# Where the low halves of three weight tensors are subtracted on GpSimd in a two-layer transformer kernel

## The chip, the cores and the metric

The kernel runs on one core of a Trainium2 chip. The metric is the device time of one execution in microseconds, the median of three. A core has the matrix engine TensorE (PE in the profile, its weight loads PEld), the vector engine VectorE (DVE), the activation engine ScalarE (ACT), GpSimd (POOL), and SyncE (SP), which here issues DMAs. Each engine works through its own list of instructions in order, and semaphores join the lists.

## The reference

Input `x` is 8 batches of 512 rows of 256 values, float32. Two pre-norm layers follow each other, each an attention and a gated feed-forward (FFN):

- layer 0 attention: `x += softmax(causal(q k^T / 4)) v`, 16 heads of width 16, with `q, k, v = layernorm(layernorm(x)) * gamma + beta` times `w_qkv`
- layer 0 FFN: `x += fp4(h) wd^T`, with `h = silu(fp4(y) wg^T) * (fp4(y) wu^T)`, `y = layernorm(x)`; width 704. `fp4` rounds each block of 16 values to a grid of 8 magnitudes times a scale taken from the block's maximum. The weights are rounded in the same way
- layer 1 attention: banded (each row sees 64 rows), with biases and an output projection
- layer 1 FFN: gated, width 768, weights integers times 1/127

## The kernel before

**Halves.** [...] a tensor is split: ACT casts it to `high`, POOL subtracts `low = full - high`, and TensorE forms three products (`PAIRS`: high·high, high·low, low·high). Four sets of such low halves matter here: those of layer 0's gate, up and first input (L969, made in attention), of layer 0's down weights `wd_low` (L1209), of the FFN's inputs `fyT` for batches 1 to 7 (`split`, L289 to L295), and of layer 1's q, k and v weights (`late_weights`, L1177; the trace calls these tiles `qkv_wg` and `qkv_wu`, after the slots they use).

**Attention 0** (about 0 to 501.9 us of the trace) runs over 8 batches × 2 halves × 2 groups = 32 "quads" of four heads. In step `i` of the loop in `body`, quad `i` takes its exponentials and its weighted sums while quad `i + 2` forms scores and row maxima (L506, L517). One step has six parts `p`. `side[p]` holds what else belongs to a part: projections, transposes, finishing the quad before. The exponentials go from PE (L609) through ACT (L620) to POOL, which zeroes the masked triangle (`only`, L128), and back to PE (L674). `fill` is a generator that feeds layer 0's weight rounding into these steps. The layer 1 call of the same function has a second generator, `last_weights`, stepped in the last quads.

**FFN 0** (501.9 to about 800 us) runs over 32 tiles of 128 rows, `n` in the code, four to a batch. Step `n` turns the rows of tile `n-3` (PE L1246, ACT L1250, DVE L1251), forms gate and up for tile `n` (24 matmuls at L1227, ACT silu L1233, DVE product L1234), starts rounding tile `n` (`quantize`: DVE L221, L227, L228, then POOL L229), multiplies tile `n-3` by the down weights (L1260), and ends the rounding of tile `n-1` (ACT L277, DVE L279 and L281, POOL L282). `prepare(b)`, advanced twice a step, normalizes, rounds, transposes and splits the inputs of the next batch, `fy` and then `fyT`. `late_weights` is advanced once a step from `n = 6` on. Its first three steps make the halves of layer 1's q, k and v weights; then it loads `wd2_i`.

**What sets the order.** The framework's scheduler orders each engine's list by its own estimate of when things are ready and how urgent they are; it may move an instruction far from where the program has it. `keep_in_program_order` (called `pin` too) puts an edge from the instruction traced last on the same engine to this one, so that it can't be issued before that. It adds no wait on a result. A tile pool's buffers are known by tags; a new tile with the tag of an old one waits until that is no longer used. The pool `fp` of the FFN takes the memory of attention's pool `ap`, and its first tiles wait for attention's end. `wp` lives through both.

Before the change `wd_high` lies in `wp` under the tag `raw`, in the place of `qkv_raw`, which attention's last projection reads at 440.2 us. `wd_low` lies in `fp`.

Of the kernel before, what the change touches and what calls it, by code (L numbers as in the profile page):

```python
# [10 lines left out]
F32 = mybir.dt.float32  # L11
BF16 = mybir.dt.bfloat16
F32R = mybir.dt.float32r
# [3 lines left out]
ALU = mybir.AluOpType  # L17
AX = mybir.AxisListType

P = 128  # L20
B, S, D = 8, 512, 256
# [25 lines left out]
def tile_two_layers(  # L47
# [22 lines left out]
    nc = tc.nc  # L70
# [4 lines left out]
    wp = tc.alloc_tile_pool(name="weights0", bufs=1, side="right")  # L75
# [23 lines left out]
    qkv_raw = wp.tile([P, NE, 3 * D], F32, tag="raw", name="qkv_raw")  # L99
# [73 lines left out]
    def pin(ins):  # L173

        tc.keep_in_program_order(ins)
# [113 lines left out]
    def split(pool, hi, lo, src, name):  # L289

        n = src.free_size()
        full = pool.tile([P, 512], F32, tag="full", name=f"full_{name}", bufs=1)[:, :n]
        nc.scalar.copy(hi, src)
        nc.scalar.copy(full, src)
        nc.gpsimd.tensor_tensor(lo, full, hi.bitcast(F32), ALU.subtract)  # L295

    def project(dst, lhs, rhs):

# [58 lines left out]

    QK = [units_tiles(qk, n, "both") for n in range(2)]

    def attention(home, banded, stats, norm, spin, wq_s, wk_s, wv_s, qcol, kcol, bv_bc, post, filler):  # L360

# [91 lines left out]
        def load_q(u):  # L455
            HALF[u, 0] = pieces(*u, wq_s, qcol, "q")
# [287 lines left out]
        def body():  # L744

            q, k = units_tiles(home[0], 2, int(banded))
            QQ.append(q)
            KK.append(k)
            padded_values(home[0], 1, nc.gpsimd)
            if banded:  # L750
                for n in range(2):
                    v = home[0].tile([P, NT, H, HP], F32, tag=f"vq{n}", name=f"vq{n}", bufs=1)
                    nc.gpsimd.memset(v[WIN:, 0], 0.0)
                    VQ.append(v)
                shifted(0)
                fine = fine_halves(home[0])
                next(fine)
            norm(1)
            for i in range(1 if banded else 0, 2):
                for s in scores(i):  # L760
                    s()
                maxima(i)
            max_rows(0)
            for c in range(NE):
                turned(1, c)
            load_q(units[2])
            stores(units[2], 0)
            load_k(units[2])
            stores(units[2], 1)
            land(units[2])  # L770


            last = trail = None
            ending = filler(home[0]) if banded else None
            for i in range(len(quads) + (2 if banded else 1)):
                ts, ss, cur = [], [], None
                if i < len(quads):
                    cur = Outputs(i)
                    ts = cur.tiles()
                    if i + 2 < len(quads):  # L780
                        ss = scores(i + 2)
                c, r = i // 4, i % 4
                nT = 2 if banded else 6
                side = {p: [] for p in range(nT)}

                def at(p, fn):
                    side[p].append(fn)

                p1, p2, p3 = (1, 0, 0) if banded else (1, 2, 3)
                f1, f2, f3 = (0, 1, 1) if banded else (0, nT - 2, nT - 1)  # L790
                if banded and i + 1 < len(quads):
                    at(p3, lambda: max_rows(i + 1))

                if last is not None:
                    at(p1, lambda: last.banded_sums() if banded else last.sums((2, 3)))
                    at(p1, lambda: last.copy())
                done = trail if banded else last
                if done is not None and not banded:
                    at(p2, lambda: done.finish())

                if r == 0 and c + 1 < B:
                    at(f2 if banded else f1, lambda: values(c + 1, 0))
                if r == (2 if banded else 0) and c + 1 < B:
                    at(f1 if banded else f2, lambda: values(c + 1, 2))
                if r == 2 and c + 2 < B:
                    at(f3 if banded else f1, lambda: turned(c + 2, 0))
                    at(f3, lambda: turned(c + 2, 1))
                if r == 0 and c + 2 < B:
                    at(f3, lambda: stats(c + 2))
                if r == 1 and c + 2 < B and not banded:  # L810
                    for t in range(NT):
                        at(t, lambda t=t: norm(c + 2, [t]))
                if banded and r == 3 and c + 1 < B:
                    at(f1, lambda: shifted(c + 1))
                if r % 2 and i // 2 + 3 < len(units):
                    at(f1, lambda: load_q(units[i // 2 + 3]))
                    at(f2, lambda: load_k(units[i // 2 + 3]))
                    at(f3, lambda: stores(units[i // 2 + 3], 0))
                for p, fn in tail.pop(i, ()) if banded else ():
                    at(p, fn)  # L820
                if done is not None and banded:
                    at(p2, lambda: done.finish())
                if i + 1 < len(quads) and not banded:
                    at(p3, lambda: max_rows(i + 1))
                if cur and not banded:
                    at(f3, lambda: cur.sums((0, 1)))
                if r == 1 and c + 2 < B and banded:
                    for t in range(NT):
                        at(t // 2, lambda t=t: norm(c + 2, [t]))
                if r % 2 == 0 and i and i // 2 + 2 < len(units):  # L830
                    at(f1 if banded else p1, lambda: stores(units[i // 2 + 2], 1))
                    at(f1 if banded else f2, lambda: land(units[i // 2 + 2]))
                for p in range(max(len(ts), nT if last or done else 0)):
                    if p < len(ss):
                        ss[p]()
                        step()
                    if p < len(ts):
                        ts[p]()
                        step()
                    for fn in side[p]:  # L840
                        fn()
                    if banded and p:
                        next(fine, None)
                    if banded and i > 4 * B - 6:
                        next(ending, None)
                if ss:
                    maxima(i + 2)
                last, trail = cur, last
            for _ in ending or ():
                pass  # L850
            for n in sorted(tail) if banded else ():
                for p, fn in tail.pop(n):
                    fn()
# [6 lines left out]
    NH = (F1 + P - 1) // P  # L860
    wd1 = wp.tile([P, NH, D], F32, tag="wd1", name="wd1")
# [111 lines left out]
    HALVES = {}  # L973
    wqp = tc.alloc_tile_pool(name="wquant", bufs=1, side="right")
    with tc.tile_pool(name="attn0", bufs=2) as ap:
# [6 lines left out]
        fill = before_ffn(wqp)  # L982
# [15 lines left out]
        def spin0(b, c, dst):  # L998
            transposed(dst, Y[b], f"a{b}", [c], (gcol, bcol), True)

        def post0(b, c, o, rz):
            tmp = ap.tile([P, NT, 4, HD], F32, tag="on", name=f"on_{b}_{c}")
            nc.vector.tensor_tensor(tmp, o, rz, ALU.mult)
            xs = X[b][:, :, c * 64 : (c + 1) * 64]
            nc.gpsimd.tensor_tensor(xs, xs, tmp.rearrange("p t j d -> p t (j d)"), ALU.add)

        opening0, body0 = attention(
            (ap, 1, 2, None), False, stats0, norm0, spin0, qkv_raw[:, :, 0:D], qkv_raw[:, :, D : 2 * D],
            qkv_raw[:, :, 2 * D : 3 * D], None, None, None, post0, fill,
        )  # L1010
        for _ in opening0():
            pass
# [9 lines left out]
    bv_bc = const.tile([P, D], F32, tag="bvb", name="bv_bc")  # L1022
# [104 lines left out]
    def last_weights(pool):  # L1127
# [24 lines left out]

    opening1, body1 = attention(
        home1, True, stats1, norm1, spin1, raw1[:, 0], raw1[:, 1], raw1[:, 2], qcol1, kcol1, bv_bc,
        post1, last_weights,
    )
    with tc.tile_pool(name="ffn0", bufs=2) as fp:
        both = []
# [10 lines left out]
        def late_weights():  # L1169
# [4 lines left out]
            ]  # L1174
            for i in range(3):
                nc.scalar.copy(halves[0][:, i], raw1[:, i])
                nc.gpsimd.tensor_tensor(  # L1177
                    halves[1][:, i], raw1[:, i], halves[0][:, i].bitcast(F32), ALU.subtract
                )
                yield  # L1180
            flat = wp.tile([P, 6 * D], I32, tag="wd1", name="wd2_i")
            nc.sync.dma_start(
# [12 lines left out]
        def prepare(b):  # L1195
# [6 lines left out]


        wd_halves = [
            wp.tile([P, NH, D], F32R, tag="raw", name="wd_high"),
            fp.tile([P, NH, D], F32R, tag="wdl", name="wd_low", bufs=1),
        ]
        nc.scalar.copy(wd_halves[0], wd1)
        nc.gpsimd.tensor_tensor(  # L1209
            wd_halves[1], wd1, wd_halves[0].bitcast(F32), ALU.subtract  # L1210
        )


        rows = [fp.tile([P, NH * P], F32, tag=f"h{i}", name=f"h{i}", bufs=1) for i in range(4)]
# [177 lines left out]
    with tc.If(nc.values_load(beyond, min_val=0, max_val=P) != 0):  # L1392
        with tc.tile_pool(name="over", bufs=1) as op:
# [10 lines left out]
            for b in range(B):  # L1404
                y = op.tile([P, NT, D], F32, tag="y", name=f"oy_{b}")
# [63 lines left out]
```

## Time and profile before

| | us |
|---|---|
| three timed runs, median | 1280.49 (1279.89 to 1282.59) |
| the profiled execution's own time | 1288.33 |
| its span in the trace | 1286.5 |
| PE busy | 1100.3 |
| DVE busy | 943.5 |
| POOL busy | 698.8 |
| ACT busy | 659.7 |

A line of the timeline reads: start in us, duration in us, engine, line of the kernel, operation, output `<-` inputs with sizes, how many (`x3`), and in brackets how long the engine had been idle and whose result ended that. When several of one kind follow each other they are merged, and the duration runs from the first start to the last end. A line of the waits reads: who waited, for whom, total in us, times, longest. A line of the windows reads: stretch, its length, busy us and count of PE, PEld, DVE, ACT and POOL, TensorE's granted clock as a share of full speed, and the DMAs' share and rate.

### The profile page before, as it was taken

To read this page: it belongs to the slowest core of one execution; us is meant where nothing else is said; L and a number is where in the kernel's file an instruction comes from. 1 tells how busy PE (TensorE), PEld (TensorE's weight loads), DVE (VectorE), ACT (ScalarE), POOL (GpSimd) and SP (SyncE) were. 2 spreads that over 40 slices of the span, in tenths; PEclk is the share of its full clock that TensorE was granted. 3 is DMA by queue.
4 is the path that set the end of the run, shared out by engine and by line. 5 is a ranking of instruction groups with operands and counts; after the bars stand their busy time and mean duration, and the time that the engine had idled before them with its cause. 6 is when DMAs were issued, how large, how long until landed. Compare 5 with 4: busy or idle time off the path is not lost. (4 is left out here: it accounts for less than half of the span.)

```text
span 1286.5 us, 27214 instructions
## 1 busy us (share of the span) xinstructions
PE 1100.3 (86%) x10910; PEld 819.8 (64%) x10910; DVE 943.5 (73%) x1603; ACT 659.7 (51%) x1008; POOL 698.8 (54%) x821
## 2 busy tenths in 40 slices
PE   4778989788998888788888887788998898889998
PEld 2444444444554445787888777567777776668887
DVE  4699896698788885789799857677776686545553
ACT  3255656465674676444444333455555554455553
POOL 5165564465445566655555533576766675534443
PEclk9899999898998999899999988899999998999999
DMA  8644334443453311000000025476675676000001
GB/s 229 140 96 87 86 74 86 79 94 67 91 116 74 81 18 50 1 1 1 1 1 1 1 72 105 100 165 155 144 149 125 141 164 163 2 1 33 33 26 43
DMA packets 51634, 99.53 MB, mean 77 GB/s; under 512 B 6702, under 2 KB 43568, under 8 KB 44848
## 3 DMA queue, kind: packets, MB, share of 16 engines
q1 hardware_dynamic: 50624, 96.96, 33.9%
q8 instruction: 88, 1.44, 0.5%
q10 hardware_dynamic: 816, 0.79, 0.2%
q14 instruction: 42, 0.34, 0.1%
q0 software_dynamic: 64, 0.00, 0.0%
HBM read 61.02 MB, written 29.36 MB: 70 GB/s over the span
## 5 line engine op out<-in xcount | busy, mean ns | idle before, releaser
L128 POOL TENSOR_SCALAR_AFFINE_SELECT ex<-ex 64x512 f32<-64x512 f32 (+2 forms) x448 | 268.9, 603 | 226.1 <-ACT ex L620 131.3
L620 ACT ACTIVATE ex<-t 128x1024 f32<-128x1024 f32 (+1 forms) x192 | 167.9, 882 | 125.3 <-PE t L609 114.1
L517 DVE TENSOR_REDUCE mx<-s 128x2 f32<-128x1024 f32 (+2 forms) x192 | 196.7, 1036 | 41.1 <-PE s L506 40.3
L1319 POOL TENSOR_TENSOR hT<-gh,hT 128x512 fp32r<-128x512 f32 x48 | 61.6, 1290 | 89.6 <-ACT hT L1318 66.1
L655 ACT ACTIVATE ex<-t 128x1024 f32<-128x1024 f32 x64 | 65.5, 1023 | 86.6 <-PE t L647 81.9
L501 PE MATMUL s<-kk_both,qq_both 96*128 96x512 bf16 (+3 forms) x352 | 84.6, 323 | 20.8 <-DVE mx L517 10.9
L506 PE MATMUL s<-cmask,minus_b 128*128 128x128 bf16 (+2 forms) x352 | 90.4, 257 | 0.0
L540 DVE TENSOR_REDUCE mx<-s 128x8 f32<-128x1024 f32 x64 | 77.6, 1215 | 15.3 <-PE s L535 15.2
L282 POOL TENSOR_TENSOR h<-h,sc_h 128x704 f32<-128x704 f32 x32 | 45.1, 1410 | 79.4 <-DVE h L281 73.6
L674 PE MATMUL po<-ex,vp 128*32 128x512 f32 (+3 forms) x1024 | 83.4, 442 | 1.3 <-DVE kr L418 1.3
L609 PE MATMUL t<-qq_both,kk_both 108*128 108x512 bf16 (+3 forms) x352 | 70.9, 306 | 9.1 <-ACT ex L620 4.7
L1386 DVE SCALAR_TENSOR_TENSOR gh<-ggu,gsl 128x512 f32<-128x512 f32 x48 | 33.2, 691 | 57.1 <-ACT gsl L1384 56.6
L1260 PE MATMUL pd<-wd_high,hT 128*128 128x256 f32 x384 | 61.7, 299 | 11.6 <-DVE hT L1251 7.0
L277 ACT ACTIVATE mg_h<-h 128x704 bf16<-128x704 f32 x32 | 25.2, 788 | 82.7 <-POOL h L229 82.7
L1227 PE MATMUL gu<-wg_wgh,fyT 128*128 128x352 f32 x224 | 65.3, 333 | 2.4 <-DVE h L1234 2.4
L501 PEld LDWEIGHTS <-qq_both 96*128 96x128 bf16 x352 | 33.0, 103 | 51.6 <-issue 38.0
L229 POOL TENSOR_TENSOR h<-h,rc_h 128x704 f32<-128x704 f32 x32 | 46.4, 1449 | 34.1 <-DVE rc_h L228 18.8
L1260 PEld LDWEIGHTS pd<-wd_high,hT 128*128 128x128 f32 x384 | 53.7, 200 | 16.4 <-DVE hT L1251 10.7
L1227 PE MATMUL gu<-wu_wuh,fyT 128*128 128x352 f32 x224 | 62.7, 322 | 0.0
L1375 PE MATMUL ggu<-yT,wg_r 128*128 128x512 f32 x192 | 57.6, 412 | 2.1 <-DVE yT L1319 1.1
L279 DVE SCALAR_TENSOR_TENSOR h<-mg_h,h 128x704 f32<-128x704 bf16 x32 | 40.6, 1269 | 22.4 <-ACT mg_h L277 22.4
L674 PEld LDWEIGHTS po<-ex,vp 128*32 128x32 f32 x1024 | 27.1, 109 | 43.9 <-issue 29.8
(335 smaller groups left out, 3167.9 us busy)
## 6 DMA issues: line engine op xcount, KB each, us to landing
q_hbm<-qp SPq DMA_DIRECT2D x90, 128.0 KB
k_hbm<-kp SPq DMA_DIRECT2D x90, 128.0 KB
qq_both<-q_hbm SPq DMA_DIRECT2D x44, 256.0 KB
kk_both<-k_hbm SPq DMA_DIRECT2D x22, 384.0 KB
qq_both<-q_hbm SPq DMA_DIRECT2D x44, 128.0 KB
kk_both<-k_hbm SPq DMA_DIRECT2D x22, 256.0 KB
qq<-q_hbm SPq DMA_DIRECT2D x20, 256.0 KB
vq<-vp SPq DMA_DIRECT2D x8, 512.0 KB
```

The source lines that it names most:

```text
L128: nc.gpsimd.affine_select(out=t, in_=t, compare_op=ALU.is_ge, fill=0.0, base=base, pattern=[[0, n] for n in shape[1:-1]] + [[sign, shape[- ...
L501: pin(nc.tensor.matmul(bank[:, a * w : (a + 1) * w], lhsT=q[:KF, hs[j], t * P : w], rhs=k[:KF, hs[j], :w], start=(a == 0), stop=False, ski ...
L506: pin(nc.tensor.matmul(bank.rearrange("p (i k) -> p i k", k=w)[:, :, t * P :], lhsT=minus_b, rhs=cmask[:, : len(part), :], start=False, st ...
L517: nc.vector.tensor_reduce(dst, src, AX.X, ALU.max)
L540: nc.vector.tensor_reduce(mx[:, t2 : t2 + 2, :], sc.rearrange("p t (j k) -> p t j k", k=P), AX.X, ALU.max)
L609: pin(nc.tensor.matmul(bank[:, a * w : (a + 1) * w], lhsT=k[: KF + 12, self.hs[j], t * P : (t + 1) * P], rhs=q[: KF + 12, self.hs[j], t * ...
L620: nc.scalar.activation(ex[:, :banks, :used], sc[:, :banks, :used], AF.Exp, scale=QSCALE)
L655: nc.scalar.activation(ex, sc, AF.Exp, scale=QSCALE)
L674: pin(nc.tensor.matmul(self.o[HP * j : HP * (j + 1), t * P :], lhsT=vp[:, t, 4 * c + j, :], rhs=self.ex[t, j], start=(t == 0), stop=(t == ...
L1227: nc.tensor.matmul(gu[:, i, :352], lhsT=YT[b][l][:, e, t * P : (t + 1) * P], rhs=w[r][:, e, f], start=(n == 0), stop=(n == 3 * NE - 1),)
L1260: nc.tensor.matmul(pd[:, :D], lhsT=hT[l][:, k, :], rhs=wd_halves[r][:, k, :], start=(l == r == k == 0), stop=(l == 1 and k == NH - 1),)
L1319: engine.tensor_tensor(lo, src, hi.bitcast(F32), ALU.subtract)
```

## The change

`attention` gets one more argument, a generator stepped in its last quads; layer 0 is given the new `down_low`, layer 1 its `last_weights` as before. `down_low` makes `wd_low` in three pieces of two 128-row blocks each. For each piece ACT casts `wd1` into a high copy that is used for this alone (in the slot of attention's normalized rows, tag `y`, one buffer), and POOL subtracts it. `wd_low` lies in `wp` under the tag `raw` now. `wd_high`, which the matmuls read, moves from `wp` to `fp`, and the large subtraction at the FFN's start goes. The subtraction in `split` and those of layer 1's weights are pinned.

```diff
@@ split
-        nc.gpsimd.tensor_tensor(lo, full, hi.bitcast(F32), ALU.subtract)
+        tc.keep_in_program_order(
+            nc.gpsimd.tensor_tensor(lo, full, hi.bitcast(F32), ALU.subtract)
+        )
...
@@ attention
-            ending = filler(home[0]) if banded else None
+            ending = last_weights(home[0])
...
-                    if banded and i > 4 * B - 6:
+                    if i > 4 * B - 6 and (banded or p == 2):
                         next(ending, None)
...
-            for _ in ending or ():
+            for _ in ending:
                 pass
...
+        def down_low(pool):
+
+            low = HALVES["wd"] = wp.tile([P, NH, D], F32R, tag="raw", name="wd_low")
+            for k in range(0, NH, 2):
+                high = pool.tile([P, 4, D], F32R, tag="y", name=f"wd_high_{k}", bufs=1)[:, :2]
+                nc.scalar.copy(high, wd1[:, k : k + 2])
+                nc.gpsimd.tensor_tensor(
+                    low[:, k : k + 2], wd1[:, k : k + 2], high.bitcast(F32), ALU.subtract
+                )
+                yield
...
@@ late_weights
-                nc.gpsimd.tensor_tensor(
+                pin(nc.gpsimd.tensor_tensor(
                     halves[1][:, i], raw1[:, i], halves[0][:, i].bitcast(F32), ALU.subtract
-                )
+                ))
...
@@ ffn0
         wd_halves = [
-            wp.tile([P, NH, D], F32R, tag="raw", name="wd_high"),
-            fp.tile([P, NH, D], F32R, tag="wdl", name="wd_low", bufs=1),
+            fp.tile([P, NH, D], F32R, tag="wdh", name="wd_high", bufs=1), HALVES["wd"]
         ]
         nc.scalar.copy(wd_halves[0], wd1)
-        nc.gpsimd.tensor_tensor(
-            wd_halves[1], wd1, wd_halves[0].bitcast(F32), ALU.subtract
-        )
```

## The prediction, made before the changed kernel was run

> **What bounds the kernel now.** I read the windows by stage first, then the waits of the stretch where attention hands over to the FFN, then the timelines of each engine there. The chain of work that ended last is of no use: it names only the last two instructions. The windows (PE, PEld, DVE, ACT and POOL busy, then the granted clock):
>
> ```profile
> 464.00:474.60 10.60, 9.26 (x84) 4.95 (x83) 8.83 (x17) 7.72 (x11) 9.61 (x12) 1.00 0.00 0
> ...
> 484.00:491.00 7.00, 6.08 (x60) 2.77 (x56) 1.24 (x4) 5.64 (x7) 2.41 (x6) 1.00 0.00 0
> ...
> 501.90:534.60 32.70, 21.49 (x118) 20.51 (x117) 26.49 (x41) 16.61 (x29) 26.30 (x21) 0.79 0.17 49
> 534.60:568.60 34.00, 31.61 (x222) 30.52 (x221) 29.42 (x43) 15.62 (x27) 18.75 (x14) 1.00 0.01 1
> ```
>
> In the FFN's steady course (last row) PE is busy 31.6 of 34.0 us. In its first 32.7 us it is busy 21.5 and half as many matmuls go through, at a clock of 0.79, while POOL is busy 26.3. The waits from 495 to 545 us say for whom:
>
> ```profile
> PE ph L1246 <- POOL h L282: 5.2, 1, 5.2
> ...
> PE pt_f L937 <- POOL fy L282: 3.0, 1, 3.0
> ...
> PE gu L1227 <- DVE h L1234: 3.0, 1, 3.0
> ```
>
> That is 11.2 us in which PE stands still, two of the three behind POOL. POOL's timeline there:
>
> ```profile
> 501.93 3.51 POOL L1209 TENSOR_TENSOR wd_low<-wd,wd_high 128x1536 fp32r<-128x1536 f32 x1
> ...
> 507.76 1.94 POOL L229 TENSOR_TENSOR fy<-fy,rc_x 128x1024 f32<-128x1024 f32 x1 [0.97 <-DVE rc_x L228]
> 509.66 4.75 POOL L1177 TENSOR_TENSOR qkv_wu<-raw,qkv_wg 128x512 fp32r<-128x512 f32 x3
> 514.37 2.37 POOL L229 TENSOR_TENSOR h<-h,rc_h 128x704 f32<-128x704 f32 x1
> 516.70 1.93 POOL L282 TENSOR_TENSOR fy<-fy,sc_x 128x1024 f32<-128x1024 f32 x1
> 520.31 1.90 POOL L229 TENSOR_TENSOR h<-h,rc_h 128x704 f32<-128x704 f32 x1 [1.69 <-DVE rc_h L228]
> 522.18 1.26 POOL L295 TENSOR_TENSOR fyT<-full_f,fyT 128x512 fp32r<-128x512 f32 x1
> 523.40 2.03 POOL L282 TENSOR_TENSOR h<-h,sc_h 128x704 f32<-128x704 f32 x1
> ```
>
> All three kinds of operation that the diff touches (`wd_low`, `qkv_wu`, `fyT`) stand ahead of the product at 523.40 for which PE waits. They slow DVE too:
>
> ```profile
> 503.68 2.16 DVE L155 TENSOR_SCALAR ve_f<-mv_f 128x4 f32<-128x4 f32 x1
> ...
> 510.90 2.35 DVE L279 SCALAR_TENSOR_TENSOR fy<-mg_x,fy 128x1024 f32<-128x1024 bf16 x1
> ...
> 541.54 1.23 DVE L279 SCALAR_TENSOR_TENSOR fy<-mg_x,fy 128x1024 f32<-128x1024 bf16 x1 [0.85 <-ACT mg_x L277]
> ```
>
> The first ends 0.4 us after `wd_low` does, for an operation on four values a row (0.17 us elsewhere); the second takes 2.35 us beside `qkv_wu`, 1.23 with POOL idle.
>
> **What the Trainium skill says.** (1) "SBUF — State Buffer", section "Who interferes with whom": a DVE instruction with two SBUF inputs, or in a two-port mode, shares a port pair with GpSimd instructions that read SBUF, and the later one blocks until the other is done. The rows above agree. (2) "TensorE: Matmul & The Clock Gate", Part 1: TensorE falls to half rate after an idle window of about 3.4 us and returns after as long a busy one. The trace agrees: matmuls follow each other 0.29 us apart from 508.9 and from 526.7 us, after the pauses, and 0.16 us apart otherwise. (3) "GPSIMD Engine Reference", section 3: about 2.6 cycles an element for two inputs at 1.2 GHz, so an estimate of 1.11 us for 512 elements before dispatch; the trace has 1.26 to 1.29 alone, 2.1 beside DVE, and I use the trace.
>
> **The change, part by part.**
>
> *`wd_low` leaves the FFN's start* (−3.51 us of POOL). `ve_f` drops from 2.16 to about 0.17. The maximum of `fy` can start when `fy` is normalized: 503.97, not behind `ve_f` at 505.84. Then 1.21 (maximum) + 0.16 + 0.19 + 0.55 (L162, L227, L228) put POOL's L229 at 506.1, not 507.76: −1.65. PE's first wait ends with DVE's L1234, which stood behind these; its silu is ready at 506.1, so PE goes on at about 506.6, not 508.11: −1.5.
>
> *`wd_high` moves to the start.* It ran on ACT under attention:
>
> ```profile
> 440.68 1.48 ACT L1208 CAST wd_high<-wd 128x1536 fp32r<-128x1536 f32 x1
> ...
> 501.89 2.08 ACT L168 ACTIVATE fy<-x,mr_f,rs_f 128x256 f32<-128x256 f32 x4 [2.47 <-POOL x L1005]
> 503.99 1.28 ACT L1233 ACT_TABLE_LOAD   x1
> ```
>
> Now its tile needs attention's memory, so 501.9 is the earliest. Its 1.48 us cost up to −1.5's whole gain if they stand ahead of the four normalizations; nothing in ACT's pauses (1.55 us at 506.6, 2.5 at 514.3), as its first reader is due at 531.9. Being less urgent than `fy`, it should go to a pause: I take 0.3. The load of `wd2_i`, which waited for `wd_low`, waits for this cast instead; SP has nothing queued behind it there.
>
> *The `qkv` subtractions leave* (−4.75 us of POOL). L279 of `fy` falls from 2.35 to 1.23 (−1.1), L229 of tile 0 no longer waits 0.8 (reciprocal ready 513.59, start 514.37) and falls from 2.37 to 1.39. With the 1.5 before, DVE's L281 of `fy` ends near 512.9 (was 515.49), and POOL's L282 of it near 515 (was 518.63). PE, restarted at 506.6, has 36 matmuls in 7.6 us, to 514.2. So `pt_f` starts near 515, not 518.68: −3.7.
>
> *`split` is pinned.* Its first subtraction was at 522.18, ahead of tile 0's L282. In program order, L229 of tile 2 precedes it. So L282 of tile 0: L229 ends near 512.5, ACT 0.8, DVE L279 and L281 0.88 each behind L221 of tile 1, to 516; POOL, after L282 of `fy` and L229 of tile 1, starts it at 517 and ends at 518.5 (was 525.43). Its matmuls then start near 518.6, not 525.48: −6.9. `fyT` is due at tile 4's first matmul, 534.6 before and 527.7 then; tile 2's L229 can end near 521, two splits and L282 of tile 1 (1.26 × 2 + 1.39) reach 525.
>
> Each time here leans on the one before, and the list's order is the scheduler's. I take −6 for the start. Bounds: −2 (0.8 of the wait and 1.26 of the split, no more) and −12 (all 11.2 us and some of the slow clock).
>
> *Three pieces under attention.* Three casts of 128×512 (0.59 us each, the row of L293) against one of 1.48 gone: +0.3 us of ACT, which is idle 1 to 2 us at a time. Three subtractions on POOL, 1.27 to 2.1 each: 3.8 to 6.3 us. From 440 to 464 and in 484 to 491 POOL is busy half or less; from 464 to 474.6 it is busy 9.6 of 10.6 with other halves. What waits behind a piece is L128's masking, then PE's L674. PE's weight loads waited 3.4 us in all for it from 440 to 500, so it isn't free. All on the path: +4 to +6; all in gaps: 0. I take +1.
>
> *`qkv` comes back in steps 6 to 8.* Pinned behind `fyT` of batch 2, POOL's pauses of 2.4 us at 566 and 5.3 at 574.7 take it:
>
> ```profile
> 580.03 1.39 POOL L282 TENSOR_TENSOR h<-h,sc_h 128x704 f32<-128x704 f32 x1 [5.29 <-DVE h L281]
> ```
>
> Cost 0 in pauses, up to 4.8 (3 × 1.58) otherwise. I take 0.5.
>
> *The pin in the other six batches.* The first split moves from 591.86 behind L229 of tile 10 (598.10), the second from 596.04 to about 601; the first matmul of the next batch is some 10 us later. ACT's second copy waits for the first split (one `full` buffer), with the hidden tile's cast behind it:
>
> ```profile
> 559.52 0.59 ACT L294 COPY full_f<-pt_f 128x512 f32<-128x512 f32 x1 [2.04 <-POOL fyT L295]
> 560.00 0.81 ACT L1250 CAST hT<-ph 128x768 fp32r<-128x768 f32 x1
> ```
>
> If that wait vanishes, up to −1 a batch; if it lengthens by the 6 us and isn't reordered, up to +2. I take 0.
>
> Sum: −6 + 0.3 + 1 + 0.5 = −4.2, against the profiled execution's span of 1286.5: 1282.3. Its own time, 1288.33, is 1.8 more than the span, and 7.8 above the median of the timed runs; I carry the difference over: 1280.5 − 4.2 = 1276.3. Nothing downstream takes it back, since FFN and attention 1 follow the same PE list. The measurement can tell about 0.2% (2.6 us) from no change.
>
> **Rivals.**
>
> *Faster by more*: the start gives 9 or more and the pins 0.5 a batch: about −11, 1269. For it: 11.2 us of pauses plus lost clock. Against it: DVE, 26.5 of 32.7 us busy, becomes the start's bound.
>
> *No change*: the start gives 3, because the new order on DVE or the cast ahead of `fy` holds the chain, and the pieces cost 2 to 3 under attention: 1280. For it: attention's masking is on PE's path. That the pieces or the `qkv` subtractions do not move as the program says belongs here: where the scheduler keeps the pieces to attention's end, POOL's time at the start is the same.
>
> *Slower*: the pinned split holds ACT. In each of seven batches the second copy waits for a first split that comes up to 6 us later, and tile casts and silus queue behind it. At 0.75 us a batch it cancels a net 5; at 1.5 us it gives +10.5 − 4.2 = +6, 1286. For it: 10.5 us of this wait already, six times. Against it: the scheduler knows the one buffer and can place the copy later; the hidden tile's L282 is relieved of a split ahead of it.
>
> **How the numbers follow.** Forecast (−2.6 to −9): 0.50. Much faster: 0.10. No change: 0.14. Slower: 0.26. So faster 0.60, same 0.14, slower 0.26. Single-case range 1271 to 1278. For 8 in 10 I go from 1270 (within the much-faster case) to 1285 (most of the slower one).
>
> **What would show it.** Right: no L1209 on POOL and three 128×512 subtractions between 440 and 500 us; `ve_f` under 0.3 us; L279 of the first `fy` near 1.25; PE's wait for POOL's L282 near 1 us where it was 5.2; the first `pd` matmuls near 526 (was 531.9), attention's end within 1 us of 501.9; batches of 34.0 us in the FFN after that. Wrong: `wd_high` ahead of the first `fy`; attention's end 3 us later; a longer wait of L294 for L295; PE's gap before `ph` turning into one before tile 4 for `fyT`.

## The result, and the profile after

The changed kernel is slower: 1289.66 us (median of 20 runs, 1284.44 to 1295.34) against 1282.49 us for the kernel before on the same chip (20 runs, 1277.20 to 1290.30). The ratio is 1.0051, with a 95% interval of 1.0035 to 1.0067. On the 1280.49 us of the prediction that is 1287.0, outside its range of 1270 to 1285. The profiled execution took 1290.39 us, with a span of 1288.7. Here and below a ratio and its interval are estimated from the single runs, so a ratio need not be the quotient of the two medians beside it.

Lines have moved: the subtraction in `split` is L296 (was L295), the pieces of `wd_low` L1009, their casts L1008, the cast of `wd_high` L1220 (was L1208), layer 1's `qkv` subtractions L1190 (was L1177), gate and up L1236 (L1227), silu L1242 (L1233), the product L1243 (L1234), the turning of tiles L1255, L1259 and L1260 (L1246, L1250, L1251), the down matmuls L1269 (L1260). The timelines below are excerpts: `...` stands for lines left out; where only lines of other engines lie between two, there is no mark.

First the FFN's start. The windows of the stretch from attention's end to tile 4's first matmul, and of the 35.6 us that follow (columns as before):

```profile
498.10:526.60 28.50, 20.45 (x119) 19.64 (x118) 21.91 (x38) 17.81 (x30) 16.20 (x16) 0.88 0.17 56
526.60:562.20 35.60, 30.82 (x213) 29.25 (x212) 28.31 (x41) 14.51 (x26) 19.21 (x14) 1.00 0.00 1
```

The start is 4.2 us shorter (32.70 before), POOL's work in it has fallen from 26.3 to 16.2 us, and the granted clock has risen from 0.79 to 0.88. The second row has the loss in it: PE is busy 30.8 of 35.6 us, where it was 31.6 of 34.0. The timeline of the start:

```profile
438.66 1.27 POOL L1009 TENSOR_TENSOR wd_low<-wd,wd_high 128x512 fp32r<-128x512 f32 x1 [0.73 <-ACT wd_high L1008]
...
498.13 1.48 ACT L1220 CAST wd_high<-wd 128x1536 fp32r<-128x1536 f32 x1 [2.46 <-POOL x L1018]
499.52 2.07 ACT L168 ACTIVATE fy<-x,mr_f,rs_f 128x256 f32<-128x256 f32 x4
...
499.92 0.17 DVE L155 TENSOR_SCALAR ve_f<-mv_f 128x4 f32<-128x4 f32 x1
...
503.74 1.94 POOL L229 TENSOR_TENSOR fy<-fy,rc_x 128x1024 f32<-128x1024 f32 x1 [1.05 <-DVE rc_x L228]
...
506.80 1.23 DVE L279 SCALAR_TENSOR_TENSOR fy<-mg_x,fy 128x1024 f32<-128x1024 bf16 x1 [0.64 <-ACT mg_x L277]
...
511.06 1.93 POOL L282 TENSOR_TENSOR fy<-fy,sc_x 128x1024 f32<-128x1024 f32 x1 [1.23 <-DVE fy L281]
513.05 1.09 PE L939 MATMUL pt_f<-ident,fy 128*128 128x128 f32 x8 [1.51 <-POOL fy L282]
...
516.55 1.38 POOL L282 TENSOR_TENSOR h<-h,sc_h 128x704 f32<-128x704 f32 x1
517.98 1.54 PE L1255 MATMUL ph<-ident,h 128*128 128x128 f32 x6 [3.84 <-POOL h L282]
```

`wd_low` is made under attention (its three subtractions take 1.27 to 1.28 us each and lie from 436.7 us on), `ve_f` takes 0.17 us instead of 2.16, L279 1.23 instead of 2.35, and POOL has none of the three kinds of operation that the diff touches ahead of the product for `ph`. But `wd_high`'s cast stands ahead of the four activations that normalize `fy`.

Then the steady course. The waits from 545 to 780 us, in the kernel before:

```profile
ACT full_f L294 <- POOL fyT L295: 10.5, 6, 2.0
...
DVE h L1234 <- ACT sl L1233: 5.4, 6, 1.4
...
PE gu L1227 <- DVE h L1234: 2.4, 3, 1.1
```

and in the changed one:

```profile
ACT full_f L294 <- POOL fyT L296: 21.7, 6, 5.1
...
DVE h L1243 <- ACT sl L1242: 17.5, 10, 3.5
...
PE gu L1236 <- DVE h L1243: 8.3, 9, 1.6
```

ACT's second copy of a batch's inputs waits twice as long in all for the first subtraction. One by one the six waits are 5.1, 4.8, 2.2, 4.6, 4.6 and 0.5 us, where the kernel before has five of 2.0 and one of 0.2. The timeline of all engines at the first of these six places shows what that holds up:

```profile
555.85 1.39 POOL L229 TENSOR_TENSOR h<-h,rc_h 128x704 f32<-128x704 f32 x1 [0.65 <-DVE rc_h L228]
...
557.20 1.28 POOL L296 TENSOR_TENSOR fyT<-full_f,fyT 128x512 fp32r<-128x512 f32 x1
...
558.51 0.59 ACT L294 COPY full_f<-pt_f 128x512 f32<-128x512 f32 x1 [5.07 <-POOL fyT L296]
559.00 0.60 ACT L168 ACTIVATE fy<-x,mr_f,rs_f 128x256 f32<-128x256 f32 x1
...
559.50 0.45 ACT L1242 ACTIVATE sl<-gu 128x352 f32<-128x352 f32 x1
...
559.98 0.52 DVE L1243 TENSOR_TENSOR h<-sl,gu 128x352 f32<-128x352 f32 x1 [3.47 <-ACT sl L1242]
...
560.56 0.43 PE L1236 MATMUL gu<-wg_wgh,fyT 128*128 128x352 f32 x1 [1.32 <-DVE h L1243]
```

The pin keeps the subtraction behind L229. There is one `full` buffer, so the copy waits for it, 5.07 us. ACT works in order, so a silu whose matmuls ended at 556.4 (the start of the last is 556.11) comes at 559.50. DVE's product waits for the silu, and PE's next gate and up matmuls wait for the buffer that the product frees.

### The profile page after: what moved, and what is told of

The parts are those of the page before. It is cut to its first block, busy times and chain, and to the rows that moved or that the text cites. A ratio compares the mean times of both kernels' runs of the same rounds, so it can differ in the third digit from the quotient of the medians.

```text
span 1288.7 us, 27213 instructions
## 1 busy us (share of the span) xinstructions
PE 1095.7 (85%) x10910; PEld 815.1 (63%) x10910; DVE 939.8 (73%) x1603; ACT 661.0 (51%) x1011; POOL 693.8 (54%) x823
## 5 line engine op out<-in xcount | busy, mean ns | idle before, releaser
L1328 POOL TENSOR_TENSOR hT<-gh,hT 128x512 fp32r<-128x512 f32 x48 | 61.7, 1291 | 90.1 <-ACT hT L1327 66.3
L503 PE MATMUL s<-kk_both,qq_both 96*128 96x512 bf16 (+3 forms) x352 | 82.4, 316 | 22.6 <-DVE mx L519 12.6
L282 POOL TENSOR_TENSOR h<-h,sc_h 128x704 f32<-128x704 f32 x32 | 44.5, 1389 | 87.0 <-DVE h L281 81.2
L1269 PE MATMUL pd<-wd_high,hT 128*128 128x256 f32 x384 | 61.8, 299 | 14.2 <-DVE hT L1260 8.7
L1236 PE MATMUL gu<-wg_wgh,fyT 128*128 128x352 f32 x224 | 65.9, 336 | 8.3 <-DVE h L1243 8.3
L229 POOL TENSOR_TENSOR h<-h,rc_h 128x704 f32<-128x704 f32 x32 | 45.4, 1419 | 39.3 <-DVE rc_h L228 27.0
L1269 PEld LDWEIGHTS pd<-wd_high,hT 128*128 128x128 f32 x384 | 53.8, 199 | 19.2 <-DVE hT L1260 12.3
L277 ACT ACTIVATE mg_h<-h 128x704 bf16<-128x704 f32 x32 | 25.2, 786 | 78.1 <-POOL h L229 78.1
L1236 PE MATMUL gu<-wu_wuh,fyT 128*128 128x352 f32 x224 | 63.1, 324 | 0.0
L279 DVE SCALAR_TENSOR_TENSOR h<-mg_h,h 128x704 f32<-128x704 bf16 x32 | 41.0, 1282 | 20.7 <-ACT mg_h L277 20.7
L676 PEld LDWEIGHTS po<-ex,vp 128*32 128x32 f32 x1024 | 27.2, 110 | 43.9 <-issue 29.1
```

Source lines behind the costliest of these rows:

```text
L503: pin(nc.tensor.matmul(bank[:, a * w : (a + 1) * w], lhsT=q[:KF, hs[j], t * P : w], rhs=k[:KF, hs[j], :w], start=(a == 0), stop=False, ski ...
L676: pin(nc.tensor.matmul(self.o[HP * j : HP * (j + 1), t * P :], lhsT=vp[:, t, 4 * c + j, :], rhs=self.ex[t, j], start=(t == 0), stop=(t == ...
L1236: nc.tensor.matmul(gu[:, i, :352], lhsT=YT[b][l][:, e, t * P : (t + 1) * P], rhs=w[r][:, e, f], start=(n == 0), stop=(n == 3 * NE - 1),)
L1269: nc.tensor.matmul(pd[:, :D], lhsT=hT[l][:, k, :], rhs=wd_halves[r][:, k, :], start=(l == r == k == 0), stop=(l == 1 and k == NH - 1),)
L1328: engine.tensor_tensor(lo, src, hi.bitcast(F32), ALU.subtract)
```

## How the stages compare

Attention's last addition to `x` starts anywhere from 497.4 to 504.7 us in single profiled executions, with the same instruction order up to 420 us in all of them, so spans of one execution can't be compared to a microsecond. I take times from the start of that addition instead: to PE's first matmul after its first pause, to the first `pt_f`, the first `ph` and tile 4's first matmul, and then to the start of DVE's last silu product of batches 0, 1, 2 and 7.

| kernel | PE goes on | `pt_f` | `ph` | tile 4 | batch 0 | batch 1 | batch 2 | batch 7 |
|---|---|---|---|---|---|---|---|---|
| before | 7.0 | 17.6 | 24.4 | 33.5 | 31.5 | 65.8 | 100.0 | 278.8 |
| after | 6.7 | 15.7 | 20.6 | 29.2 | 29.4 | 66.2 | 102.7 | 287.7 |
| e1_split_free | 6.7 | 15.7 | 22.5 | 31.3 | 29.3 | 64.9 | 100.1 | 277.6 |
| e2_split_pin_alone | 7.0 | 17.7 | 22.6 | 32.5 | 30.5 | 67.1 | 102.7 | 286.5 |
| e3b_two_copies | 6.7 | 15.7 | 20.6 | 29.7 | 28.3 | 64.6 | 99.4 | 278.0 |
| e4_first_batch_pinned | 6.7 | 15.7 | 20.6 | 29.8 | 29.4 | 65.0 | 100.2 | 278.6 |
| e5_wd_low_alone | 6.7 | 17.3 | 24.1 | 34.0 | 32.0 | 66.3 | 100.6 | 278.2 |
| e6_qkv_pin_alone | 7.0 | 16.0 | 22.8 | 32.6 | 30.6 | 66.1 | 101.3 | 279.1 |
| e8_spaced | 6.7 | 15.7 | 20.6 | 30.4 | 28.3 | 63.3 | 96.4 | 273.6 |
| e9_spaced_two_copies | 6.7 | 15.7 | 20.6 | 29.2 | 27.3 | 62.9 | 96.0 | 273.9 |
| e10_cast_behind_fy | 5.4 | 14.0 | 18.9 | 27.8 | 27.2 | 61.1 | 94.2 | 272.5 |
| e11_wd_low_cast_behind_fy | 5.4 | 17.1 | 24.6 | 34.1 | 32.0 | 66.6 | 100.8 | 279.6 |

After minus before is −2.1 us at the end of batch 0 and +9.0 at the end of batch 7. The timed runs of whole executions give +6.5 (0.51% of 1280.5). The 2.5 us between the two aren't accounted for; the stages come from one execution of each kernel.

## The experiments

### Which part loses the time

The theory is the held copy: the pin on `split` delays the first subtraction, the one `full` buffer passes the delay to ACT's queue, and ACT passes it to DVE and PE. The rivals are that the other parts cost it (the pieces under attention, the `qkv` subtractions in steps 6 to 8), or that the pin costs through POOL's order alone, whatever ACT waits for.

**e1_split_free**: the changed kernel without the pin on `split`.

```diff
-        tc.keep_in_program_order(
-            nc.gpsimd.tensor_tensor(lo, full, hi.bitcast(F32), ALU.subtract)
-        )
+        nc.gpsimd.tensor_tensor(lo, full, hi.bitcast(F32), ALU.subtract)
```

> The changed kernel with the pin in split alone taken off. Held copy (the pin makes the first split late, ACT's second copy waits 5 us for it with a silu behind): ACT's waits of L294 for the split fall from 22 us to about 10, a batch of the FFN goes back from about 35.5 to 34 us, and the time is 0.995 of the kernel before (the start's gain, some 4 to 7 us, stays, less about 2 us because the splits stand ahead of tile 0 again). Order of POOL (late splits back to back cost by themselves): the same here. Neither (the q, k, v subtractions in steps 6 to 8 or the cast at the start cost the 10 us): still 1.004 or more.

Measured: 1282.03 us against 1281.99, ratio 0.9992 (0.9971 to 1.0014). The FFN, to batch 7, is back to 277.6 us, 10.1 less than after.

**e2_split_pin_alone**: the kernel before, with that pin as its only edit (the diff above the other way round).

> The kernel before with the pin in split alone put on. Held copy and order of POOL both: slower than before by 7 to 12 us (1.006 to 1.009), with six waits of about 5 us of ACT's L294 for the split. Neither: within 0.2% of before.

Measured: 1292.13 us against 1281.99, ratio 1.0066 (1.0042 to 1.0090). The pin alone costs as much as the whole change. Its waits from 540 to 790 us are those of the changed kernel:

```profile
ACT full_f L294 <- POOL fyT L296: 20.4, 6, 5.1
DVE h L1236 <- ACT sl L1235: 18.8, 12, 3.5
...
PE gu L1229 <- DVE h L1236: 7.7, 9, 1.6
```

**e3b_two_copies**: the changed kernel with its pins, but each half of a batch's inputs has its own full copy, so that the second copy has nothing to wait for. This is the run that separates POOL's order from the wait.

```diff
-    def split(pool, hi, lo, src, name):
+    def split(full, hi, lo, src, name):
-        n = src.free_size()
-        full = pool.tile([P, 512], F32, tag="full", name=f"full_{name}", bufs=1)[:, :n]
...
+            copies = wp.tile([P, NE, S], F32, tag="fyT", name=f"full_f{b}")
...
-                split(pool, yT[0][:, c, :], yT[1][:, c, :], pt, f"f{b}_{c}")
+                split(copies[:, c], yT[0][:, c, :], yT[1][:, c, :], pt, f"f{b}_{c}")
```

> The changed kernel, pins kept, but each half of a batch's inputs has its own full copy, so ACT's second copy waits for no split. Held copy: the batches go back to about 34 us and the time is 0.993 to 0.996 of before, as with the pin off or better. Order of POOL: still 1.004 or more, with no wait of L294.

Measured: 1282.04 us against 1281.99, ratio 1.0000 (0.9979 to 1.0022), the FFN 278.0 us. No wait of L292 (the copy) for the subtraction is left in the stretch. ACT's timeline at the place of the 5.07 us wait:

```profile
555.48 0.59 ACT L292 COPY full_f<-pt_f 128x512 f32<-128x512 f32 x1
556.66 0.80 ACT L1258 CAST hT<-ph 128x768 fp32r<-128x768 f32 x1 [0.59 <-PE ph L1254]
557.36 1.10 ACT L168 ACTIVATE fy<-x,mr_f,rs_f 128x256 f32<-128x256 f32 x2
558.58 0.47 ACT L1241 ACTIVATE sl<-gu 128x352 f32<-128x352 f32 x1
```

The copy is done ahead of the tile's cast, and nothing stands still behind it. POOL's order is still that of the pin: in five of the six batches both subtractions stand behind L229, as in the changed kernel (in the second of the six the first one stands ahead of it). So the held copy is shown: the pin without the wait costs nothing that shows, and the pin with it costs all. The six waits fall into batches 1 to 6. There, after minus e1_split_free is 1.3, 1.3, 1.2, 2.2, 2.2 and 0.3 us, 8.4 in all, and e2_split_pin_alone minus before is 9.3. ACT's idle time doesn't give the loss by itself: in batch 3 it is 2.2 us (0.9 in e2_split_pin_alone) for a loss of 1.2, in batch 1 it is 5.1 for 1.3. In batch 3 the scheduler put more ahead of the copy, and what is late behind it is `mg_h` (L277), not a silu. The last batch has no such wait; its 1.6 us more are not put down to the pin, since its length lies anywhere from 43.1 to 44.5 us in the other kernels, which don't differ there.

### Where the start's gain went

Without the held copy the kernels are still not faster than before, where the expectations had 0.993 to 0.996. That leaves a second question: the start's 2 to 4 us.

**e4_first_batch_pinned**: the changed kernel, with `split`'s pin for batch 1 alone, which is the one that the start is meant to gain from.

```diff
-        tc.keep_in_program_order(
-            nc.gpsimd.tensor_tensor(lo, full, hi.bitcast(F32), ALU.subtract)
-        )
+        low = nc.gpsimd.tensor_tensor(lo, full, hi.bitcast(F32), ALU.subtract)
+        if name.startswith("f1_"):
+            tc.keep_in_program_order(low)
```

> The changed kernel with the pin in split kept for the first batch only, where it lets tile 0 go ahead. Held copy: the six later batches lose their 5 us waits, so 0.993 to 0.996 of before, some 1 to 3 us under the kernel with no pin in split. If the pin costs at the start too: no faster than the kernel with no pin in split.

Measured: 1281.99 us against 1281.99, ratio 0.9999 (0.9980 to 1.0018). `ph` comes 1.9 us earlier than in e1_split_free (20.6 against 22.5) and tile 4 1.6 us earlier, but by the last product of batch 0 nothing of it is left (29.4 against 29.3). The traces show where it goes, in the changed kernel and here alike. In the changed kernel:

```profile
523.69 1.02 POOL L160 TENSOR_TENSOR rs_f<-ve_f,mhalf 128x4 f32<-128x4 f32 x1
...
524.26 0.47 ACT L1242 ACTIVATE sl<-gu 128x352 f32<-128x352 f32 x1
...
524.75 1.25 DVE L162 SCALAR_TENSOR_TENSOR mr_f<-mv_f,rs_f 128x4 f32<-128x4 f32 x1 [1.51 <-POOL rs_f L160]
...
526.73 0.51 DVE L1243 TENSOR_TENSOR h<-sl,gu 128x352 f32<-128x352 f32 x1
```

`rs_f` and `mr_f` belong to the normalizing of a later batch's inputs. The last product of batch 0 is DVE's L1243 at 526.73. Its silu has ended at 524.73, but DVE has `mr_f` and then an L279 ahead of the product; `mr_f` waits 1.51 us for `rs_f`, and takes 1.25 us beside POOL's second subtraction (0.16 in the kernel before). The product comes 2.0 us behind its silu, and 1.7 us in e4_first_batch_pinned; in e1_split_free it is 0.03 us. No run changes that order alone, so this is read from the traces and not tested.

In the next two batches more is lost: the 2.1 us of lead over before at batch 0 have become a lag of 0.2 at batch 2. The timeline of the kernel before, where the first `qkv` subtraction will stand:

```profile
566.06 0.16 DVE L162 SCALAR_TENSOR_TENSOR mr_f<-mv_f,rs_f 128x4 f32<-128x4 f32 x1 [2.55 <-POOL rs_f L160]
...
567.51 0.43 PE L1227 MATMUL gu<-wg_wgh,fyT 128*128 128x352 f32 x1 [0.42 <-DVE h L1234]
```

and that of e4_first_batch_pinned:

```profile
566.53 1.28 POOL L1190 TENSOR_TENSOR qkv_wu<-raw,qkv_wg 128x512 fp32r<-128x512 f32 x1
567.77 1.00 POOL L160 TENSOR_TENSOR rs_f<-ve_f,mhalf 128x4 f32<-128x4 f32 x1
568.81 0.16 DVE L162 SCALAR_TENSOR_TENSOR mr_f<-mv_f,rs_f 128x4 f32<-128x4 f32 x1 [3.79 <-POOL rs_f L160]
...
570.26 0.43 PE L1236 MATMUL gu<-wg_wgh,fyT 128*128 128x352 f32 x1 [1.67 <-DVE h L1243]
...
584.14 2.27 POOL L1190 TENSOR_TENSOR qkv_wu<-raw,qkv_wg 128x512 fp32r<-128x512 f32 x1
586.38 1.94 POOL L282 TENSOR_TENSOR fy<-fy,sc_x 128x1024 f32<-128x1024 f32 x1
```

The first subtraction stands ahead of `rs_f`, for which DVE is waiting already, and PE's wait grows by as much as the subtraction takes (0.42 to 1.67). The third, which takes 2.27 us while DVE's L281 runs (1.28 for the first), stands ahead of L282 of `fy`. Only the second, at 577.46, lies in a pause.

**e6_qkv_pin_alone**: the kernel before with only the three `qkv` subtractions pinned.

```diff
-                nc.gpsimd.tensor_tensor(
+                pin(nc.gpsimd.tensor_tensor(
                     halves[1][:, i], raw1[:, i], halves[0][:, i].bitcast(F32), ALU.subtract
-                )
+                ))
```

> The kernel before with only the three qkv subtractions pinned, so that they leave the start for steps 6 to 8. Theory (they cost 2.3 us in steps 6 to 8): the start 2 to 4 us shorter, the first two batches together 2 us longer than before, ratio 0.999 to 1.000. Rival (the pauses take them, as predicted): the first two batches as before, ratio 0.997 to 0.998.

Measured: 1283.20 us against 1282.73, ratio 0.9999 (0.9980 to 1.0018). The lead is 0.9 us at batch 0, and at batch 2 it is a lag of 1.3: the move costs 2.2 in steps 6 to 8, as expected, and the start gained less than the 2 to 4 us expected.

**e8_spaced**: e4_first_batch_pinned, with the three subtractions in steps 7, 11 and 15, each behind L229 of `fy`, where POOL then stands idle for 5 us. All that `late_weights` does afterwards moves along, DVE's conversion and maximum of layer 1's down weights too (0.95 and 1.69 us, from 596 and 607 us in the kernel before to 654 and 659).

```diff
-            if n >= 6:
+            if n in (7, 11, 15) or n > 15:
                 next(lw, None)
```

> The changed kernel, split's pin for the first batch alone, and the three qkv subtractions in steps 7, 11 and 15 of the FFN instead of 6, 7 and 8 (what follows them moves along), each behind a POOL subtraction after which POOL stands idle for about 5 us. Theory (the place in steps 6 and 8 costs 2.3 us): the first two batches within 0.6 us of before's together, the start 3 to 4 us shorter than before's, ratio 0.997 to 0.998. Rival (the start's gain is not worth anything at the end): ratio 1.000 as for the kernel with only the first batch pinned.

Measured: 1279.18 us against 1282.73, ratio 0.9964 (0.9948 to 0.9981). POOL's and DVE's timeline at the same places:

```profile
562.26 1.01 POOL L160 TENSOR_TENSOR rs_f<-ve_f,mhalf 128x4 f32<-128x4 f32 x1
563.30 0.17 DVE L162 SCALAR_TENSOR_TENSOR mr_f<-mv_f,rs_f 128x4 f32<-128x4 f32 x1 [2.54 <-POOL rs_f L160]
...
571.94 1.29 POOL L1190 TENSOR_TENSOR qkv_wu<-raw,qkv_wg 128x512 fp32r<-128x512 f32 x1
577.28 1.39 POOL L282 TENSOR_TENSOR h<-h,sc_h 128x704 f32<-128x704 f32 x1 [4.04 <-DVE h L281]
579.89 1.94 POOL L282 TENSOR_TENSOR fy<-fy,sc_x 128x1024 f32<-128x1024 f32 x1 [1.23 <-DVE sc_h L227]
```

`mr_f` waits 2.54 again, as before, and the subtraction at 571.94 is followed by 4.04 us of idleness: it costs nothing there. So the place was what cost, and the start is worth its time at the end. The FFN is 5.0 us shorter than e4_first_batch_pinned's: 1.1 by batch 0, where `mr_f` no longer holds the last product up (it comes 0.03 us behind its silu), 2.7 in batches 1 and 2, 0.3 in batches 3 to 6, and 0.9 in the last batch, which varies by as much anyway. Of the 2.7, 2.2 is what e6_qkv_pin_alone shows for the place; the other 0.5 isn't separated from DVE's moved work.

**e9_spaced_two_copies**: e8_spaced with the two full copies of e3b_two_copies.

> The same as e8_spaced, and each half of a batch's inputs has its own full copy, so that no second copy waits for a first subtraction. Theory (only a wait that the pin has lengthened costs anything; the 10.5 us of it that the kernel before has are covered): the same as e8_spaced within 0.1%. Rival (a wait of 2 us costs PE in proportion, as one of 5 us does): 0.5 us a batch, 3 us less than e8_spaced, ratio lower by 0.002.

Measured: 1277.12 us against 1282.73, ratio 0.9951 (0.9935 to 0.9967). The FFN takes 273.9 us against e8_spaced's 273.6, and the two intervals overlap, so this doesn't decide between the two expectations by time. By the stages the waits of 2.0 to 2.6 us, 12.9 us in all in e8_spaced, cost nothing that shows: batches 2, 3, 5 and 6 are equally long in both kernels to 0.02 us, and 1 and 4 are not shorter without the waits.

### What wd_low alone is worth, and the cast ahead of fy

**e5_wd_low_alone**: the changed kernel without both pins, so that only `wd_low` and `wd_high` move (the diffs of e1_split_free and of e6_qkv_pin_alone the other way round).

> The changed kernel without both pins: only wd_low goes under attention and wd_high to the FFN's start. Theory (the cast ahead of fy eats the gain): the start is 1 to 2 us shorter than before, the rest of the FFN as before, attention without a cost that shows: ratio 0.998 to 1.000. Rival (the three pieces cost attention the 4 to 6 us of the prediction's upper bound, and this takes the start's gain back in the free-split kernel too): ratio 1.002 or more. Rival (the start's gain comes from this part): start 3 to 4 us shorter, ratio 0.997.

Measured: 1285.05 us against 1282.73, ratio 1.0018 (0.9998 to 1.0038). The start is not shorter: tile 4 at 34.0, batch 0 at 32.0 (33.5 and 31.5 before), so the theory's 1 to 2 us are not there. Its ratio is nearer to the rival of a cost under attention (1.002 or more), and the interval decides between neither; e11_wd_low_cast_behind_fy, with the same pieces, speaks against that cost.

**e11_wd_low_cast_behind_fy**: the same, with the cast of `wd_high` traced and pinned behind the first `mg_x` (L277).

```diff
-        nc.scalar.copy(wd_halves[0], wd1)
...
                     for _ in range(3):
                         next(ahead)
+                    pin(nc.scalar.copy(wd_halves[0], wd1))
```

> Only wd_low under attention and wd_high in the FFN's memory, both pins off, with the cast of wd_high behind mg_x of the first fy. Theory: PE goes on 4.7 us after attention's last addition (6.2 in the kernel before, 5.96 with the cast ahead of fy), the start 1 to 1.5 us shorter than before's 33.5, ratio 0.999. Rival (qkv and split still stand ahead of the product that PE waits for, so POOL's queue keeps the end of the start where it was): start 33 to 34 us, ratio 1.000 to 1.002.

Measured: 1283.01 us against 1284.03, ratio 0.9995 (0.9982 to 1.0008). PE goes on 5.4 us after the addition's start, 1.6 earlier than before. (This expectation and the next count PE's restart and `pt_f` from the addition's end, some 0.75 us later, so their 4.7 is this 5.4.) But `ph` is at 24.6 and tile 4 at 34.1, as the rival said: PE waits the time out in front of POOL.

```profile
507.57 0.43 PE L1233 MATMUL gu<-wg_wgh,y_wg 128*128 128x352 f32 x1 [1.40 <-DVE h L1240]
...
519.23 1.97 PE L937 MATMUL pt_f<-ident,fy 128*128 128x128 f32 x8 [5.66 <-POOL fy L282]
...
526.76 1.54 PE L1252 MATMUL ph<-ident,h 128*128 128x128 f32 x6 [5.56 <-POOL h L282]
```

**e10_cast_behind_fy**: e9_spaced_two_copies with the same edit. The `qkv` subtractions don't stand in POOL's queue at the start here; the scheduler also changed the order of some DVE and POOL operations.

> The kernel with spaced qkv subtractions and two copies, and the cast of wd_high placed on ACT behind mg_x (L277) of the FFN's first fy instead of ahead of fy; the scheduler also changes the order of a few DVE and POOL operations behind that. Theory (the cast ahead of fy takes the 1.5 us that the prediction counted): PE goes on 4.7 us after attention's last addition to x instead of 5.96, pt_f's first matmul at 13.6 us instead of 14.9, the start 1.2 us shorter, ratio 0.994. Rival (DVE's order, not the cast, sets the start): PE goes on at 4.7 us but pt_f and ph come as late as before, start unchanged, ratio 0.995.

Measured: 1277.04 us against 1284.03, ratio 0.9950 (0.9930 to 0.9970), not to be told from e9_spaced_two_copies by time. In the stages the 1.3 us are there at PE's restart, and 1.7 at `pt_f` and `ph`. At the last product of batch 0, where `mr_f` stands ahead of it again, 0.1 is left; 1.8 are there at batch 1, and 1.4 at batch 7 (272.5 against 273.9):

```profile
507.34 0.43 PE L1234 MATMUL gu<-wg_wgh,y_wg 128*128 128x352 f32 x1 [1.31 <-DVE h L1241]
...
509.92 1.46 ACT L1286 CAST wd_high<-wd 128x1536 fp32r<-128x1536 f32 x1
...
515.87 1.09 PE L938 MATMUL pt_f<-ident,fy 128*128 128x128 f32 x8 [2.53 <-POOL fy L282]
...
520.81 1.54 PE L1253 MATMUL ph<-ident,h 128*128 128x128 f32 x6 [3.85 <-POOL h L282]
```

The cast lies behind `mg_x`, not in either of the pauses that the prediction had named, and holds nothing of `fy` up. By the stages the same move gains only where nothing else holds the start's end. This kernel, e8_spaced and e9_spaced_two_copies are faster than the kernel before, by 0.4 to 0.5%.

## Why the prediction was wrong

**The step that failed** is "The pin in the other six batches", at the words "if it lengthens by the 6 us and isn't reordered, up to +2. I take 0." In five of the six batches it lengthened by 2.0 to 3.0 us, and it wasn't reordered far enough: at the place shown the scheduler moved the second copy behind one activation and the tile's cast, and the silu behind it still came late. The pin costs 8.4 to 9.3 us over the six batches, 1.2 to 2.3 in all but the last of them. The rival "the pinned split holds ACT" had the mechanism and the place. That its total of 1286 us is so near the 1287.0 of the measured ratio is partly luck: it counted 1.5 us in seven batches where six pay 1.4 to 1.6 on average, and took −4.2 for all the rest, where the stages have about 0 (−2.1 for the start, +2.2 for `qkv`). What spoke against it in the prediction, that the scheduler can place the copy later, should have carried less: the same trace showed the scheduler leaving that wait in place six times.

**The start: mechanism right, size off.** The prediction said −6 at tile 4, from −1.5 at PE's restart, −3.7 at `pt_f` and −6.9 at `ph`. The changed kernel has −0.3, −1.9, −3.7 and −4.3. The mis-sized term up to there is `wd_high`: 0.3 was put down for it in a pause, and it stood ahead of `fy`; moving it behind `mg_x` (e10_cast_behind_fy against e9_spaced_two_copies) gives 1.3 at PE's restart and 1.7 at `ph`. With that e10_cast_behind_fy has −1.6, −3.6, −5.5 and −5.7, close to the predicted chain. But tile 4's first matmul was the wrong place to read the gain. In the changed kernel it starts 0.1 us ahead of DVE's last product of batch 0, in the kernel before 2.0 us behind it, and at that product the changed kernel's lead is 2.1 us. The prediction followed the chain to PE and had no term for `mr_f`, which holds that product 2.0 us; e9_spaced_two_copies, with the cast still ahead of `fy` but nothing holding the product, leads by 4.2. The steps also don't add up one by one. `wd_low` alone gives nothing, with the cast ahead of `fy` or behind it, while `qkv` and `split` still stand on POOL ahead of PE's product.

**`qkv` in steps 6 to 8**: 0.5 was taken, 2.2 measured. The pauses named (2.4 us at 566 and 5.3 at 574.7) are there, but the pins put only one subtraction of three into one. In e8_spaced all three stand behind L229 of `fy`, and the 5.3 us pause takes them at no cost that shows.

**The pieces under attention**: +1 was taken, 4 to 6 as the upper bound. No run shows such a cost: attention's last addition starts at 501.0 us on average in the nine kernels with the pieces and at 502.4 in the three without, where single executions differ by up to 7.4. Less than that isn't settled; e5_wd_low_alone's ratio leaves room for up to 1.0038, and e11_wd_low_cast_behind_fy's, with the same pieces, for 1.0008. (From 440 to 464 us POOL was busy 13.0 of 24 us, a little over the half that the prediction read there; nothing rests on it.)

**The carrying over** of the profiled execution's own time to the median did no harm. Of what the prediction listed as signs, `ve_f`, L279, the three pieces and the missing subtraction at the start came as described; of its signs of being wrong, `wd_high` ahead of `fy` and the longer wait of L294 came, and a gap of PE ahead of tile 4 did not. PE's wait for POOL's L282 ahead of `ph` fell from 5.2 to 3.8 us, not to 1, since PE arrived earlier too.

## What to carry to other kernels

A tie that only orders one engine moves every instruction that waits for its result. Follow the tied result to its reader, and if that reader sits in an in-order queue over a single buffer, count what stands behind it: here waits longer by 2 to 3 us cost 1.2 to 2.3 us a batch, while waits of 2 us with other work behind them cost nothing that showed. A second buffer took that cost away.

An operation moved off a busy stretch gains only if its new place is read from the timeline as exactly as the old one: the pause must lie directly behind the instruction that it is tied to. And where several operations hold the same end, one of them taken away alone may give nothing. Read the gain at the end of the stretch, on every engine: 4.3 us at a matmul were 2.1 us at the next product.

## What was unexpected of the hardware

The Trainium skill ("TensorE: Matmul & The Clock Gate", Part 1) has TensorE's rate fall after an idle window of some 3.4 us. In these runs shorter pauses were enough at times, that of 2.96 us in the kernel before too, which the prediction read as agreement, and the length alone didn't decide. After the same first pause of 2.70 us, matmuls were 0.29 us apart from the second on in the changed kernel, and 0.16 us apart throughout in e5_wd_low_alone and e8_spaced. After the same 2.62 us there was no slow stretch in e1_split_free and one from the fifth or sixth matmul on in e3b_two_copies and e4_first_batch_pinned. Each slow stretch was ten to twelve matmuls, some 3.3 us, long. No first pause of 1.31 or 1.40 us was followed by one.

The granted clock of the traces shows what decided. In each of the twelve it changes only at points that lie 3.41 us or a multiple of it apart, so time falls into windows of 3.41 us, and a pause can fill most of one or be split between two. Here are the windows from the changed kernel's first pause on, and then those of e1_split_free:

```profile
500.42:503.83 3.41, 0.98 (x7) 0.68 (x5) 2.17 (x5) 3.38 (x7) 1.11 (x2) 1.00 0.94 306
503.83:507.25 3.42, 3.16 (x11) 3.16 (x12) 2.58 (x6) 2.81 (x5) 1.85 (x1) 0.50 0.20 69
...
502.63:506.04 3.41, 2.12 (x14) 1.83 (x12) 1.83 (x6) 3.39 (x6) 1.02 (x1) 1.00 0.82 235
506.04:509.45 3.41, 2.08 (x13) 2.08 (x14) 3.17 (x9) 2.80 (x7) 1.94 (x1) 1.00 0.63 223
```

In the changed kernel PE is busy 0.98 us of the first window, and the next has a clock of 0.50. In e1_split_free the pause is split, PE is busy 2.12 and 2.08 us, and the clock stays at 1.00. Over all windows of the twelve traces that ran at full clock, each one with PE idle for more than 57% of it was followed by half the clock, and none with PE idle for less than 36%; between the two, both occurred. So it was the share of such a window that counted, not a whole idle one.

It cost the start little here: `pt_f` comes 15.7 us after the addition in e1_split_free, without a slow stretch ahead of it, and in the changed kernel, with one, since both wait for `fy`.
